# Edge tables built by node on ScalarE, and a group's product and sums moved within the step, in a graph attention and mixture-of-experts kernel

## The chip, the core and the metric

One Trainium2 chip, one of its cores. The metric is device time of the whole kernel in microseconds; smaller is better. Engines are named as in the profile: PE (TensorE matmul), PEld (its weight load), DVE (VectorE), ACT (ScalarE), POOL (GpSimd), SP (SyncE, which here issues most DMAs).

## What is computed

6250 nodes with 256 features, 100,000 edges sorted by target node `dst`, so that a target's edges lie together. First a graph attention layer with 8 heads, then a routed feed-forward net with 8 experts of which each node uses 2. Cut to what matters here:

```python
h = (layer_norm(x) @ W).reshape(N, 8, 32)
e = leaky_relu(a_src[src] + a_dst[dst], 0.2)        # per edge and head
ee = exp(e - emax[dst])
agg = segment_sum(h[src] * (ee / segment_sum(ee, dst)[dst])[:, :, None], dst)
out = layer_norm(agg + xn @ W_res + bias)
x = x + out + gelu_tanh(out @ ffn_w1 + b1) @ ffn_w2 + b2   # per node
x = x + sum over the node's 2 experts of weight * expert(layer_norm(x))
```

Targets are drawn so that few edges per node lie at high node numbers and many at low ones.

## The kernel before

**Preparation (to about 121 us).** Node features go through the first norm and the product with `W`; per tile of 128 nodes a row of 256 features and 16 source factors goes to the DRAM table `tab_s`, and 16 target factors to `tab_d`, of which `tab_q` is an overlapping copy in windows of 32 nodes. The edge lists are turned so that a column holds 128 edges.

**The edge loop.** Edges are worked in 196 steps of four tiles of 128 edges. A step's four tiles belong to four windows of 32 neighbouring target nodes. One to eight steps form a group, whose four windows are summed together: there are 110 groups, of one step each at high node numbers, where the loop begins, and of two, four and eight further on. By the rule that forms the groups, the first 68 steps are groups of one step. What one step needs is spread over seven turns of the loop, by the table `STAGES` (L910), which gives each function the number of turns it lags behind, in the order in which a turn writes them:

```python
STAGES = ((sum_up, 6), (weigh, 3), (add_tiles, 4), (place, 4), (turn_spread, 1), (give, 2),
          (spread, 0), (add_nodes, 5), (fetch, 0))
```

- `fetch` (L806): four indirect gathers on POOL bring the source rows of 512 edges into `gs` (four buffers).
- `spread` (L817): DVE compares each edge's place in its window with 0..31 and so makes a one-hot table `oh`, a row for each edge. In a group's first step it also makes `qd` (L828), the group's target factors `gd` laid out in four blocks by a multiplication with `quad`.
- `turn_spread` (L832): PE transposes `oh` into the PSUM tile `pt`, and ACT copies it to `oht` (L836): the same table with a row for each node. `pt` is one buffer, shared with the transposes of the tasks (`turn`, L963).
- `give` (L839): PE multiplies `oht` and `qd` and so gives each edge its target's factors, `pz`.
- `weigh` (L846): DVE multiplies source and target factors (`ww`) and then the source rows by them (`msg`, L854).
- `add_tiles` (L860): PE sums `msg` into the four windows, `pl`; behind a group's last step ACT copies it to `part` (L873).
- `place` (L884): behind a group DVE makes the one-hot table `oh2` (L887) that moves the group's 128 rows to their places in a tile of nodes. `add_nodes` (L891) multiplies by it on PE into `p2` (L894, one buffer), and `sum_up` (L898) adds `p2` into the sums of two tiles of nodes on DVE (L905).

`fetch_nodes` (L787) gathers the target factors of 32 groups at once, writes them to DRAM as `tab_g` and reads them back by SP as `gd`; four such loads serve the kernel.

**The tasks.** Between these stages a planner (`run_tasks`, L937) puts the rest of the net: products of the residual weights (L1147), the nodes' dense net (`net`, L996, with L981 and L991) as soon as all edges of two tiles are summed, the choice of experts, the scattering of nodes into expert lists `xs` (L1351, POOL), and then blocks of 256 nodes of one expert, whose weights of 1 MB each come by SP (L1396, L1397) ahead of use and whose result is added into the output by an indirect DMA (L1436, POOL). Every task has an engine, a cost in us and the tasks that it needs. In each turn of the loop the planner takes tasks in order while the engine has room; the room is `ROOM` less what `EDGES` and, behind a group's end, `BEHIND` say that the stages need. Within a turn the stages are written first and the tasks after them, and each engine executes in that written order. Expert blocks that found no room in the loop are done after its end, in a tail (53 blocks in all).

```python
ROOM = {"PE": 7.5, "DVE": 7.6, "ACT": 5.0, "POOL": 2.6, "SP": 1e9}
EDGES = {"PE": 1.3, "DVE": 2.0}
BEHIND = {"PE": 0.5, "DVE": 1.4}
```

Of the kernel before, what the change touches and what calls it, by code (L numbers as in the profile page):

```python
# [47 lines left out]
P = 128  # L51
# [6 lines left out]
G = 4  # L58
# [3 lines left out]


ROOM = {"PE": 7.5, "DVE": 7.6, "ACT": 5.0, "POOL": 2.6, "SP": 1e9}
EDGES = {"PE": 1.3, "DVE": 2.0}
BEHIND = {"PE": 0.5, "DVE": 1.4}
ROOM_AFTER = {"PE": 7.7, "DVE": 7.0, "ACT": 7.0, "POOL": 5.2, "SP": 1e9}

QUEUE = 40.0
# [149 lines left out]
def gnn_moe_kernel(  # L219
# [66 lines left out]
    NG = len(order)  # L286
    NCH = -(-EP // P)
    NCW = -(-NW // P)
    DUMMY = NP


# [25 lines left out]
    res_d = dp.tile([NP, D], F32, name="res_d")  # L317
    xp_d = dp.tile([NP, D], F32, name="xp_d")
    xt_d = dp.tile([NT, P, KD * P], F32, name="xt_d")
    xs = dp.tile([E * CAP + BT, DX], F32, name="xs")  # L320

    tab_a = dp.tile([NP + P, H], F32, name="tab_a")
# [9 lines left out]
    loct = gp.tile([P, EP], F32, name="loct")  # L332
    srce = gp.tile([P, EP], I32, name="srce")
    snloc = gp.tile([P, NQ], F32, name="snloc")
    here = gp.tile([P, 2, NQ], F32, name="here")
    kfi = gp.tile([P, NQ], I32, name="kfi")
    qrow = gp.tile([P, NCW], I32, name="qrow")
# [50 lines left out]
    nc.gpsimd.memset(blank.bitcast(I32)[:, :, D:D + 1], int(BIG))  # L388
    number = cp.tile([P, NT], I32, name="number")
    nc.gpsimd.iota(number, pattern=[[P, NT]], base=0, channel_multiplier=1)  # L390

    quad = cp.tile([P, G], F32, name="quad")
    nc.vector.memset(quad, 0.0)
    for j in range(G):
        nc.vector.memset(quad[j * W32:(j + 1) * W32, j:j + 1], 1.0)
    prm = cp.tile([P, NPR], F32, name="prm")
    pe = cp.tile([P, E, KF + 2 * KD], F32, name="pe")
    wr_sb = cp.tile([P, KD, E], F32, name="wr_sb")
# [49 lines left out]
    with ExitStack() as actx:  # L448
# [94 lines left out]
        tmp = ap_.tile([P, NCH, P], F32, name="tmp")  # L543
        nc.vector.tensor_copy(drf, drow)
        nc.vector.tensor_copy(srf, srow)
        ends = ap_.tile([P, 2, NCH], F32, name="ends")
        nc.vector.tensor_copy(ends[:, 0], drf[:, :, 0])
        nc.vector.tensor_copy(ends[:, 1], drf[:, :, P - 1])
# [67 lines left out]
        for j in range(G):  # L616
            q = slice(j * W32, (j + 1) * W32)
            nc.vector.tensor_scalar(sn[q], first[q, :, j], pcol[q], float(-j * W32), op0=ALU.add,
                                    op1=ALU.add)
        nc.vector.tensor_sub(sn, sn, kff)  # L620
        nc.vector.tensor_scalar(snloc, sn, float(P), float(-P), op0=ALU.is_ge, op1=ALU.mult)
        nc.vector.tensor_add(snloc, snloc, sn)
        nc.vector.tensor_sub(sn, first[:, :, 0], kff)
        nc.vector.tensor_scalar(here[:, 0], sn, pcol, None, op0=ALU.is_le)
        nc.vector.tensor_scalar(here[:, 1], sn, pcol, None, op0=ALU.is_gt)
# [41 lines left out]
        nc.vector.tensor_scalar(stmp, srct, float(DUMMY), good, op0=ALU.subtract, op1=ALU.mult)  # L667
        nc.vector.tensor_scalar(srce, stmp, float(DUMMY), None, op0=ALU.add)

        nc.vector.memset(acc_hi[:, NT - KHI, :], 0.0)  # L670
        nc.vector.memset(acc_hi[:, 0:2, :], 0.0)
        nc.sync.dma_start(tab_s[NP:, :], zeros[:, :DT])
# [95 lines left out]
    fb2_bc = bcast(ffn_b2[None, :], "fb2_bc", D, fp)  # L768


    GC = P // G
    cw = gnn.enter_context(tc.tile_pool(name="cw", bufs=2))
    cps = gnn.enter_context(tc.tile_pool(name="cps", bufs=1, space=PSUM))
    l2b_bc = cw.tile([P, 2, D], F32, name="o", bufs=1)
# [7 lines left out]


    live = {}
    gds = {}

    def fetch_nodes(c):  # L787

        gq = bw.tile([P, W32 * 2 * H], F32, name="gq", bufs=1)
        nc.gpsimd.indirect_dma_start(  # L790
            out=gq, out_offset=None, in_=tab_q,
            in_offset=bass.IndirectOffsetOnAxis(ap=qrow[:, c:c + 1], axis=0))
        nc.sync.dma_start(tab_g[c * P:(c + 1) * P, :], gq)
        n = min(GC, NQ - c * GC)
        gd = bw.tile([P, GC, 2 * H], F32, name="gd")
        nc.sync.dma_start(gd[:, :n], tab_g[c * P:c * P + n * G, :].rearrange(
            "(g j) (r c) -> (j r) g c", j=G, r=W32))
        gds[c] = gd

    def step_tiles(s, a):  # L800

# [14 lines left out]

    def spread(s):  # L817

        q, i = order[s]
        oh = bw.tile([P, G, W32], F32, name="oh", bufs=6)  # L820
        nc.vector.tensor_tensor(oh, jrow[:, None, :W32].to_broadcast([P, G, W32]),
                                step_tiles(s, loct)[:, :, None].to_broadcast([P, G, W32]),
                                op=ALU.is_equal)
        live[s, "oh"] = oh
        if i == 0:
            qd = bw.tile([P, G, 2 * H], F32, name="qd", bufs=3)
            gd = gds[q // GC][:, q % GC, :]
            nc.vector.tensor_tensor(qd, gd[:, None, :].to_broadcast([P, G, 2 * H]),  # L828
                                    quad[:, :, None].to_broadcast([P, G, 2 * H]), op=ALU.mult)
            live[q, "qd"] = qd  # L830

    def turn_spread(s):  # L832
        po = cps.tile([P, KD, 2 * P], F32, name="pt")
        nc.tensor.transpose(po[:, 0, :P], live[s, "oh"].rearrange("p j r -> p (j r)"), ident)  # L834
        oht = bw.tile([P, P], F32, name="oht")
        nc.scalar.activation(oht, po[:, 0, :P], AF.Copy)  # L836
        live[s, "oht"] = oht

    def give(s):  # L839

        pz = bps.tile([P, G * 2 * H], F32, name="pz", bufs=2)
        nc.tensor.matmul(pz, live.pop((s, "oht")), live[order[s][0], "qd"].rearrange(
            "p j c -> p (j c)"), start=True, stop=True)
        live[s, "pz"] = pz

    def weigh(s):  # L846
# [36 lines left out]
    @behind_group  # L883
    def place(q):  # L884

        oh2 = bw.tile([P, P], F32, name="oh2")
        nc.vector.tensor_scalar(oh2, jrow[:, :P], snloc[:, q:q + 1], None, op0=ALU.is_equal)  # L887
        live[q, "oh2"] = oh2

    @behind_group  # L890
# [7 lines left out]
    def sum_up(q):  # L898
# [4 lines left out]
        for b in range(2):  # L903
# [3 lines left out]

    STAGES = ((sum_up, 6), (weigh, 3), (add_tiles, 4), (place, 4), (turn_spread, 1), (give, 2),  # L910
              (spread, 0), (add_nodes, 5), (fetch, 0))
    LASTST = 6


# [560 lines left out]
    notes = []  # L1475
    blocks, stored, cleared, sure, chunked, moew, last_hi, ahead = [], [], [], [], [0], [], [], []
    EARLY = 10
    final_list, there = [], None
    s, u, since, was_nodes = 0, 0, [], False

    with tc.manual_schedule():
        nc.sync.dma_start(xs[E * CAP:, :].rearrange("(p r) d -> p r d", r=2), blank[:, :2])
        while s < NG + LASTST or pending or u < len(units) or len(blocks) < NS:
            for g in range(s, min(s + EARLY, NG)):
                if order[g][0] // GC not in gds:
                    fetch_nodes(order[g][0] // GC)
            for f, d in STAGES:
                if 0 <= s - d < NG:
                    f(s - d)
            if s == NG + LASTST:  # L1490
                edges.close()
            if len(firsts) < len(units) and len(firsts) <= s + 1:
                first_unit(len(firsts))
            if len(firsts) == len(units) and firsts[-1].step is not None and fp:
                first_.close()
                fp = None
            if last_hi and last_hi[0].step is not None and not moew and not fp:
                hi_pool.close()
                moew.append(ctx.enter_context(tc.tile_pool(name="moew", bufs=2, side="right")))
            nb = len(blocks) + len(ahead)  # L1500
            if moew and len(ahead) < 2 and nb < NS and any(n > nb for n, _ in sure):
                block_loads(nb)

            while sum(t.cost for t in pending if t.eng == "PE") < QUEUE:
                if (u < len(units) and units[u][2] <= s - LASTST
                        and not (ahead and was_nodes)):
                    was_nodes = True
                    node_unit(u)
                    since.append(u)
                    u += 1  # L1510
                    if u % 2 == 0 or u == len(units):
                        chunk_tasks(since, u == len(units), u == len(units) - 1)
                        since = []
                elif ahead:
                    was_nodes = False
                    block_unit(*ahead.pop(0))
                else:
                    break
            room = dict(ROOM if s < NG + LASTST else ROOM_AFTER)
            if s < NG + LASTST:  # L1520
                g = s - 5
                ends = 0 <= g < NG and order[g][1] == groups[order[g][0]][1] - 1
                for e in EDGES:
                    room[e] -= EDGES[e] + ends * BEHIND[e]
            run_tasks(s, room)
            s += 1
            if there is None and final_list and final_list[0].step is not None and len(blocks) > NS - 2:
                there = nc.values_load(total[0:1, 0:1], min_val=0, max_val=NB)
        if NS < NB:
            with tc.If(there > NS):  # L1530
                while pending or len(blocks) < NB:
                    nb = len(blocks) + len(ahead)
                    if len(ahead) < 2 and nb < NB:
                        block_loads(nb)
                    if ahead:
                        block_unit(*ahead.pop(0))
                    run_tasks(s, dict(ROOM_AFTER))
                    s += 1
# [31 lines left out]
```

## Time and profile before

| | |
|---|---|
| runs of the kernel | 2172.37, 2181.78, 2203.38 us, median 2181.78 us |
| the profiled execution | 1972.14 us, span of its instructions 1970.4 us |
| mean granted TensorE clock in it | 0.926 |
| preparation, edge loop, tail in it | 0 to 121 us, 121 to 1592 us, 1592 to 1970 us |
| PE busy | 1634.8 us (83%) |
| POOL busy | 1122.1 us (57%) |
| DVE busy | 1078.1 us (55%) |
| ACT busy | 707.7 us (36%) |

The profiled execution was about 10% shorter than the runs, so a number from the profile says how the time is made up, and not what a run takes. A line of the groups reads: source line, engine, operation, tile written and tiles read, shape and count, then busy time and mean length of one, then the idle time of the engine ahead of them and what ended it.

### The profile page before, as it was taken

What the parts mean: (1) busy time and instruction counts of PE and PEld (TensorE: products, weight loads), DVE (VectorE), ACT (ScalarE), POOL (GpSimd) and SP (SyncE); (2) the same over time, 40 slices, a digit from 0 to 9 for tenths busy, and PEclk for the clock granted to TensorE, in tenths of its full rate; (3) what the DMA queues carried; (4) which work ended last, traced back from release to release, by engine and by line L of the source; (5) the groups of instructions that cost most, each with busy time, mean ns of one, the idle gap of its engine ahead of it and who ended that gap; (6) DMA issues with size and microseconds to landing.
All of it is one profiled execution on the core that took longest, in us unless ns stands there. A gap on an engine that the chain in (4) does not pass through costs nothing. (4 is left out here: it accounts for less than half of the span.)

```text
span 1970.4 us, 28382 instructions
## 1 busy us (share of the span) xinstructions
PE 1634.8 (83%) x8533; PEld 1250.6 (63%) x8533; DVE 1078.1 (55%) x3964; ACT 707.7 (36%) x1590; POOL 1122.1 (57%) x1165
## 2 busy tenths in 40 slices
PE   4835797778787988999899997996998949999997
PEld 3523565555555766766677765775776737777775
DVE  8836878877878775565667655462453501200000
ACT  3821232322233343344434342433334314333332
POOL 2027765655655767577778777777777722112122
PEclk8968899887887999999999998998999979999999
DMA  4967664644535456566564776576776655565652
GB/s 129 290 210 225 187 202 130 184 134 146 158 112 194 152 152 170 149 199 168 179 200 136 210 206 200 155 220 201 201 232 169 205 184 131 179 186 171 196 161 57
DMA packets 245260, 348.24 MB, mean 177 GB/s; under 512 B 46465, under 2 KB 200353, under 8 KB 245100
## 3 DMA queue, kind: packets, MB, share of 16 engines
q1 hardware_dynamic: 182476, 203.56, 31.8%
q0 software_dynamic: 59312, 139.32, 27.1%
q10 hardware_dynamic: 3312, 3.48, 0.6%
q8 instruction: 70, 1.15, 0.2%
q14 instruction: 90, 0.74, 0.1%
HBM read 282.90 MB, written 67.66 MB: 178 GB/s over the span
## 5 line engine op out<-in xcount | busy, mean ns | idle before, releaser
L812 POOL DMA_INDIRECT gs<-tab_s,srce x784 | 809.9, 1033 | 363.9 <-issue 198.9
L981 PE MATMUL ph<-turned_in,w1b 128*128 128x256 f32 x1696 | 400.3, 390 | 51.2 <-ACT ht L984 38.2
L991 PE MATMUL py<-w2b,ht 128*128 128x256 f32 x1696 | 382.6, 384 | 11.7 <-DVE lg L1121 6.2
L981 PEld LDWEIGHTS ph<-turned_in,w1b 128*128 128x128 f32 x1696 | 305.2, 193 | 124.4 <-ACT ht L984 57.4
L991 PEld LDWEIGHTS py<-w2b,ht 128*128 128x128 f32 x1696 | 325.0, 193 | 58.4 <-DVE lg L1121 7.7
L1436 POOL DMA_INDIRECT out_dram<-yb,to x106 | 176.9, 1668 | 312.5 <-ACT yb L1432 124.5
L984 ACT ACTIVATE ht<-ph,pc 128x256 f32<-128x256 f32 x424 | 198.4, 473 | 206.1 <-PE ph L981 205.6
L854 DVE TENSOR_TENSOR msg<-gs,msg 128x1024 f32<-128x1024 f32 x196 | 240.5, 1227 | 6.7
L1426 DVE TENSOR_TENSOR yb<-py,b2b 128x512 f32<-128x512 f32 x53 | 36.6, 690 | 360.4 <-PE py L991 276.8
L991 PE MATMUL py<-w_sb,ht 128*128 128x256 f32 x784 | 190.5, 405 | 17.3 <-DVE lg L1121 15.0
L981 PE MATMUL ph<-turned_in,w_sb 128*128 128x256 f32 (+1 forms) x800 | 192.5, 394 | 14.2 <-ACT ht L984 14.2
L991 PEld LDWEIGHTS py<-w_sb,ht 128*128 128x128 f32 x784 | 158.7, 205 | 46.4 <-DVE lg L1121 19.6
L981 PEld LDWEIGHTS ph<-turned_in,w_sb 128*128 128x128 f32 x800 | 150.4, 200 | 44.6 <-ACT ht L984 20.3
L873 ACT ACTIVATE part<-pl 128x264 f32<-128x264 f32 x110 | 42.9, 390 | 322.3 <-PE pl L869 319.6
L836 ACT ACTIVATE oht<-pt 128x128 f32<-128x128 f32 x196 | 53.9, 275 | 271.5 <-PE pt L834 214.8
L869 PE MATMUL pl<-msg,oh 128*32 128x264 f32 x1568 | 130.9, 406 | 17.1 <-DVE msg L854 17.0
L1351 POOL DMA_INDIRECT xs<-xe,slot x98 | 103.4, 1055 | 54.3 <-DMA xs<-blank 22.1
L894 PE MATMUL p<-part,oh 128*128 128x264 f32 x220 | 84.3, 469 | 59.5 <-DVE acc_hi L905 38.8
L984 ACT ACTIVATE ht<-ph,prm 128x256 f32<-128x256 f32 (+1 forms) x200 | 92.2, 469 | 113.0 <-PE ph L981 112.6
L834 PEld LDWEIGHTS pt<-ident,oh 128*128 128x128 f32 x196 | 27.6, 141 | 138.3 <-issue 81.0
L834 PE MATMUL pt<-ident,oh 128*128 128x128 f32 x196 | 65.5, 334 | 49.6 <-ACT turned_in L973 23.1
L973 ACT ACTIVATE turned_in<-pt,pc 128x256 f32<-128x256 f32 x106 | 53.9, 559 | 134.4 <-PE pt L966 124.1
(325 smaller groups left out, 1900.8 us busy)
## 6 DMA issues: line engine op xcount, KB each, us to landing
w1b<-in_L_ffn_W_dram SPq DMA_DIRECT2D x53, 1024.0 KB
w2b<-in_L_ffn_W_dram SPq DMA_DIRECT2D x53, 1024.0 KB
xb<-xs SPq DMA_DIRECT2D x53, 260.0 KB
gs<-tab_s,srce POOLq DMA_INDIRECT x784, 3.3
b2b<-in_L_ffn_b_dram SPq DMA_DIRECT2D x53, 128.0 KB
tab_s<-hg SPq DMA_DIRECT2D x12, 544.0 KB
xg<-in_x_dram SPq DMA_DIRECT2D x12, 512.0 KB
xt_d<-xt SPq DMA_DIRECT2D x12, 512.0 KB
```

Of the source, the lines that this page charges most:

```text
L812: nc.gpsimd.indirect_dma_start(out=gs[:, j, :], out_offset=None, in_=tab_s, in_offset=bass.IndirectOffsetOnAxis(ap=srce[:, t:t + 1], axis=0))
L834: nc.tensor.transpose(po[:, 0, :P], live[s, "oh"].rearrange("p j r -> p (j r)"), ident)
L836: nc.scalar.activation(oht, po[:, 0, :P], AF.Copy)
L854: nc.vector.tensor_tensor(msg[:, :, :D].rearrange("p t (h d) -> p t h d", h=H), gs[:, :, :D].rearrange("p t (h d) -> p t h d", h=H), msg[: ...
L869: nc.tensor.matmul(pl[j * W32:(j + 1) * W32, :], oh[:, j, :], msg[:, j, :], start=i == 0, stop=last)
L894: nc.tensor.matmul(p2, oh2, part, start=True, stop=True)
L973: nc.scalar.activation(xt[:, k, :n * P], pt[:, k, :n * P], AF.Identity, bias=scale[:, KD + k:KD + k + 1], scale=scale[:, k:k + 1])
L981: nc.tensor.matmul(ph[:, :W], w1[:, k, c * P:(c + 1) * P], env["in"][:, k, :W], start=k == 0, stop=k == KD - 1)
L984: nc.scalar.activation(ht[:, :W], ph[:, :W], func, bias=b[:, c:c + 1], scale=1.0)
L991: nc.tensor.matmul(env["py"][:, j, :], env["ht", c][:, j * P:(j + 1) * P], w2[:, c, :], start=c == 0, stop=c == KF - 1)
L1351: st = nc.gpsimd.indirect_dma_start(out=xs, out_offset=bass.IndirectOffsetOnAxis(ap=slots[k][:n, t:t + 1], axis=0), in_=xes[u // 2][:n, pl ...
L1436: nc.gpsimd.indirect_dma_start(out=out, out_offset=bass.IndirectOffsetOnAxis(ap=env["to"][:, j:j + 1], axis=0), in_=env["yb"][:, j, :], in ...
```

## The change

It has four parts.

1. The table by node, `oht`, is no longer a transpose of `oh`. The target node of every edge is stored in DRAM in the preparation (`dst_d`). Each step, SP loads the four rows of 128 node numbers, each row into 32 partitions (`load_dst`, one turn ahead of `spread` and two ahead of the table), and ACT makes the table as relu(1 - |dst - node|) with two activations (`is_node`). `turn_spread` is gone, and `spread` comes one turn later.
2. `oh2` is made in the same way by ACT in place of DVE.
3. `qd` is no longer made by DVE. Three buffers of four groups' factors each are cleared once; SP loads the factors straight into the four blocks, four DMAs for four groups (`fetch_factors`). `fetch_nodes` is called at the same distance as before.
4. `sum_up` comes after `weigh`, `add_tiles`, `place`, `give` and `spread` in the turn, and `add_nodes` after the turn's tasks. `EDGES` and `BEHIND` get smaller values, so that the planner has more room for tasks.

```diff
-EDGES = {"PE": 1.3, "DVE": 2.0}
-BEHIND = {"PE": 0.5, "DVE": 1.4}
+EDGES = {"PE": 0.95, "DVE": 2.0}
+BEHIND = {"PE": 0.5, "DVE": 1.0}
...
+    node = gp.tile([P, NQ], F32, name="node")
+    qds = [gp.tile([P, GC, G, 2 * H], F32, name=f"qd{i}") for i in range(QB)]
...
+        nc.sync.dma_start(dst_d.rearrange("(c t) e -> t c e", t=P), drf)
...
+    def fetch_factors(c):
+        n = min(GC, NQ - c * GC)
+        for j in range(G):
+            nc.sync.dma_start(
+                qds[c % QB][j * W32:(j + 1) * W32, :n, j, :], bass.AP(
+                    tensor=tab_g.tensor,
+                    offset=tab_g.offset + (c * GC * G + j) * W32 * 2 * H,
+                    ap=[[2 * H, W32], [G * W32 * 2 * H, n], [1, 2 * H]]))
...
-        if i == 0:
-            qd = bw.tile([P, G, 2 * H], F32, name="qd", bufs=3)
-            gd = gds[q // GC][:, q % GC, :]
-            nc.vector.tensor_tensor(qd, gd[:, None, :].to_broadcast([P, G, 2 * H]),
-                                    quad[:, :, None].to_broadcast([P, G, 2 * H]), op=ALU.mult)
-    def turn_spread(s):
-        po = cps.tile([P, KD, 2 * P], F32, name="pt")
-        nc.tensor.transpose(po[:, 0, :P], live[s, "oh"].rearrange("p j r -> p (j r)"), ident)
+    def load_dst(s):
+        q, i = order[s]
+        t0, m = groups[q]
+        rows_ = bg.tile([P, P], F32, name="rows_")
+        nc.sync.dma_start(rows_, bass.AP(tensor=dst_d.tensor, offset=dst_d.offset + (t0 + i) * P,
+                                         ap=[[m * P, G], [0, W32], [1, P]]))
+    def is_node(out, rows_, less):
+        nc.scalar.activation(out, rows_, AF.Abs, bias=less)
+        nc.scalar.activation(out, out, AF.Relu, bias=1.0, scale=-1.0)
+    def spread_by_node(s):
+        q, i = order[s]
         oht = bw.tile([P, P], F32, name="oht")
-        nc.scalar.activation(oht, po[:, 0, :P], AF.Copy)
+        is_node(oht, live.pop((s, "rows")), node[:, q:q + 1])
...
-        nc.vector.tensor_scalar(oh2, jrow[:, :P], snloc[:, q:q + 1], None, op0=ALU.is_equal)
+        is_node(oh2, jrow, snloc[:, q:q + 1])
...
-    STAGES = ((sum_up, 6), (weigh, 3), (add_tiles, 4), (place, 4), (turn_spread, 1), (give, 2),
-              (spread, 0), (add_nodes, 5), (fetch, 0))
+    STAGES = ((weigh, 3), (add_tiles, 4), (spread_by_node, 1), (place, 4), (give, 2), (spread, 1),
+              (sum_up, 6), (load_dst, -1), (fetch, 0))
...
             run_tasks(s, room)
+            if 0 <= s - 5 < NG:
+                add_nodes(s - 5)
```

The pool `bg` of `rows_` has four buffers. In the written order of the changed kernel, 46 of the products of the expert blocks (L981, L991, of 1696 in all) and 8 of their transposes stand in the loop that stood in the tail before.

## The prediction

> **What bounds the kernel now.** I first read the span by stages, with the busy time of PE, PEld, DVE, ACT and POOL in each, since the share over the whole span mixes preparation, edge loop and tail.
>
> ```profile
> 0.00:121.00 121.00, 76.44 (x329) 53.95 (x329) 97.65 (x516) 74.10 (x206) 15.65 (x73) 0.93 0.66 206
> 121.00:200.00 79.00, 31.68 (x170) 20.20 (x170) 39.29 (x108) 7.01 (x23) 53.70 (x51) 0.72 0.78 225
> 200.00:650.00 450.00, 354.92 (x1813) 258.30 (x1811) 364.43 (x1297) 133.69 (x305) 279.15 (x302) 0.86 0.54 160
> 650.00:1200.00 550.00, 502.42 (x2776) 387.09 (x2777) 351.04 (x1267) 222.44 (x473) 401.05 (x407) 0.98 0.60 174
> 1200.00:1592.00 392.00, 347.24 (x1961) 265.24 (x1959) 181.09 (x579) 142.20 (x312) 289.41 (x271) 0.96 0.67 199
> 1592.00:1971.00 379.00, 322.05 (x1488) 265.86 (x1488) 44.62 (x199) 128.22 (x272) 83.15 (x64) 0.94 0.54 158
> ```
>
> Call the four stages of the loop A, B, C, D, and the tail E. In B, PE (79%) and DVE (81%) are equally loaded and neither is full: they wait for each other. In C and D, PE is 91% and 89% busy. POOL is fuller there than it looks: each gather is followed by some 0.3 us in which POOL waits for nothing that the profile shows.
>
> ```profile
> POOL gs L812 <- issue: 57.4, 190, 0.3
> ```
>
> That is stage D; with 8.3 us of the same kind before its other indirect DMAs, POOL is taken for 289 + 66 = 355 of 392 us. In C it is 401 + 88 = 489 of 550. A is bound by the first gathers, E by PE.
>
> Next I read the groups of instructions (page, part 5) for what the change touches, and those of the loop on DVE.
>
> ```profile
> L836 ACT ACTIVATE oht<-pt 128x128 f32<-128x128 f32 x196 | 53.9, 275 | 271.5 <-PE pt L834 214.8
> L894 PE MATMUL p<-part,oh 128*128 128x264 f32 x220 | 84.3, 469 | 59.5 <-DVE acc_hi L905 38.8
> L834 PE MATMUL pt<-ident,oh 128*128 128x128 f32 x196 | 65.5, 334 | 49.6 <-ACT turned_in L973 23.1
> ```
>
> ```profile
> L887 DVE TENSOR_SCALAR oh<-jrow,snloc 128x128 f32<-128x128 f32 x110 | 31.2, 283 | 0.0
> L828 DVE TENSOR_TENSOR qd<-gd,quad 128x64 f32<-128x64 f32 x110 | 23.9, 218 | 19.5 <-DMA gd<-tab_g 19.5
> ```
>
> PE spends 65.5 us on the transposes and stands 49.6 us before them; it stands 59.5 us before the group's product, because `p2` is one buffer and `sum_up` of the same turn has to empty it. The waits of PE in B show how much of this lies there:
>
> ```profile
> PE p L894 <- DVE acc_hi L905: 38.5, 15, 5.3
> PE p L894 <- DVE acc_lo L905: 16.4, 5, 7.1
> ```
>
> So 54.9 of B's 95.1 idle PE us are this wait. Last I read SP's own waits, because the change puts a load into its queue in every step:
>
> ```profile
> SPq L1397 <- PE py L991: 241.9, 34, 17.1
> SPq L1404 <- DMA xs<-xe,slot: 236.5, 15, 34.1
> SPq L1094 <- DVE xin L1071: 209.3, 15, 39.9
> ```
>
> SP often stands for long at the head of its queue, and what is written behind it waits too.
>
> **What the Trainium skill says.** "ScalarE: Activation LUTs", section "What ACT_TABLE_LOAD costs", prices an activation with immediate scale and bias at 186 ns + 0.833 ns for each element of the row, 93 ns more for a bias by partition, and has back-to-back ones overlap by 93 ns. For 128 elements that is 293 ns for a plain one; the copy at L836 took 275, so the trace agrees. The same page, "Table sets: the hidden batching unit", says that relu and abs are in every set: the new activations switch no table, and the written order agrees (55 table loads against 57); no trace of before shows these two functions. "DMA: Bandwidth & Descriptors", section "Queues, rings and completion order", says that SP has one row of rings and that each DMA engine takes a ring's descriptors in order. A small load behind expert weights then waits for them. The trace of before fits: after a pair of weight loads is issued (2.1 MB) SP's queue moves packets for about 10 us.
>
> **The change, part by part**, against the profiled execution of 1972 us.
>
> *Table by node.* Taken from PE: 196 transposes, 65.5 us busy (4.3, 19.3, 24.0, 17.9 in A to D), and the waits around the shared PSUM tile: 23.1 us before L834, and by the same list of waits some 8 us in C before the tasks' transposes. On ACT the copy of 0.275 us becomes two activations: abs with a bias by partition, estimate 0.39 us, and relu, 0.29 to 0.39, less 0.09 of overlap: 0.59 to 0.69, I take 0.65. So 196 x 0.38 = 74 us more on ACT, if the second adds no wait for the first (the upper bound, 0.1 us each, adds 20).
>
> *Table of the group.* 110 x 0.283 = 31 us leave DVE, and 110 x 0.65 = 72 us come to ACT. ACT's load in B goes from 134 to 134 + 57 x 0.38 + 57 x 0.65 = 193 of 450 us, in C from 222 to 273 of 550, in D from 142 to 169 of 392. It stays half idle, and the work lies after `part`, which waits for PE in any case. I price it at nothing; the cover gone (ACT late with `ht`, two buffers of `ph`), its 146 us would show in part.
>
> *Factors.* 23.9 us leave DVE. SP issues 112 DMAs instead of 4. At the start 12 of them stand ahead of the first row loads: 12 issues of about 0.5 us (L796's took 0.37, with 0.2 between issues) and one landing more. Before, the first `pz` came 5.8 us after `gd` was issued; I charge 4 us in A. Later ones come some turns early and cost nothing.
>
> *Row loads.* 196 loads of 64 KB (12.8 MB beside 348) with two turns from issue to use. Bounded above from the trace: I took the last SP issue ahead of the place where each load will stand and compared it with the moment two turns later at which ACT made that table. The median distance is 26 us, the least 3.3, and 4 of 194 are under 9 us. Four buffers hold the load back until ACT has used the one four steps before. If each load also had to wait until SP's queue next ran empty, plus 2.5 us, 18 would be late, in 11 places, 96 us of ACT's time at most, nearly all in C and D where `xb` and the weights stand ahead. Below it is nothing. I take 14 us: queues seldom have to run empty, and PE has two buffers of `ph` before it feels ACT.
>
> *Order in the turn.* `add_nodes` now stands behind the tasks, so `sum_up` has most of a turn in hand and the 58 us of waits at L894 go. In exchange `sum_up` can start only when PE has finished the turn before, and DVE's tasks stand behind it. DVE's `weigh` stands ahead of it, and PE needs only that for its next turn. So a step's DVE work has about two turns, and I charge nothing; some of the 58 us will come back as other waits between these two.
>
> *Room.* The written order moves 46 products (400.3 + 382.6 us for 1696, 0.46 each) and 8 transposes (0.27) from E into the loop: 23 us.
>
> **The sum by stages.**
> - A: 4 us longer.
> - B: PE 355 - 19 = 336, DVE 364 - 57 x 0.50 = 336. With all 61 us of removed waits gone, 336 + 95 - 61 = 370; with all of them back, 431. I take 408, since DVE is as loaded as PE: 42 us shorter.
> - C: PE 502 - 24 + 12 moved in = 490, and 28 of its 48 idle us stay: 518. POOL needs 489, so both are over 93% full; I add 6: 524, 26 shorter.
> - D: PE 347 - 18 + 11 = 340, idle 45 less 12: 373; POOL needs 355; I take 376, 16 shorter.
> - E: 23 shorter. Late rows: 14 longer.
>
> 42 + 26 + 16 + 23 - 4 - 14 = 89, so 1972 becomes 1883, a ratio of 0.955. The runs' median was 2181.78, 10.6% over the profiled execution, and no view tells why. I apply the ratio: 2083 us (taking off 89 us would give 2093).
>
> **The rivals.**
> - *Rows late.* ACT stands at its abs behind a row load that lies behind `xb` or 2.1 MB of weights, with every `ht` behind it. For: SP's waits of up to 34 us, and 32 blocks' weights loaded within the loop. Against: the median of 26 us. It cancels the other 103 us when the 32 loads cost PE over 3.2 us each; at 6 us each the profile is 1972 - 103 + 192 = 2061, the runs 2280: slower.
> - *POOL or ACT is the bound in C and D.* POOL's work is the same, so C and D give 5 us each, and B half of mine: 21 + 10 + 23 - 4 - 14 = 36, runs 2142: within 2%. For: POOL at 89 and 91% there. Against: the gathers run up to three turns ahead.
> - *The waits simply go.* B 370, C 505, D 360, no row late: 80 + 45 + 32 + 23 - 4 = 176, runs 1987. For: PE's granted clock of 0.86 in B against 0.98 in C; "TensorE: Matmul & The Clock Gate", section "Part 1: The HAM clock gate", has the clock fall after idle stretches, so fewer gaps would pay twice. Against: DVE, at 81% there, has waits of its own.
> - *The change doesn't do what it says*: the waits at L894 stay because DVE lags by more than a turn. Then only the removed work counts, about 50 us, runs 2126.
>
> **How the numbers follow.** Forecast 0.53 (2040 to 2130), waits go 0.12, POOL or ACT bound 0.20, rows late 0.11, waits stay 0.04. A difference of 2% is about what a measurement of this kernel can tell. Faster: 0.53 + 0.12 + 0.03 + a quarter of the POOL case = 0.73. Slower: 0.10. Within 2%: 0.17. The range leaves out half of the fast case and most of the slow one: 2025 to 2185.
>
> **What would show it.** Right: no wait for `sum_up` before the group's product on PE; DVE down by about 55 us; ACT up by about 146; B near 408 us and the tail near 356; no table loads around abs. Wrong: long waits of ACT for the row loads (`rows_`), PE standing before L981 for more than the 65 us (51.2 + 14.2) of the page before, or POOL without free time in C and D. A loop that takes as long as before would refute the sum.

## The result, and the profile after

The changed kernel takes 2245.65 us (median of 4 runs, 2235.97 to 2250.04), the kernel before beside it 2185.1 us (2172.37 to 2203.38): ratio 1.0267, 95% interval [1.0219, 1.0315]. It is slower; 2083 us were forecast.

Its profiled execution is one of these runs (2235.97 us, span 2234.2 us), while that of before took 1972 us. So the two profiles must not be subtracted from each other. On some chips the kernel before takes 1975 to 1977 us, on others 2155 to 2194; the runs of the result are of the second kind. I call the second kind *late chips*, for a reason shown below. Two chips of each kind were met in the experiments; only one of them was met twice, half an hour apart, and was of the first kind both times, so whether it is the chip or something of the hour is not shown. Beside e17 and e18 the kernel before spread from 2124 to 2161 us, and their ratios count its faster runs alone; by the medians of all runs they would be 1.011 and 1.002. The profile to set beside the one shown ahead is that of the changed kernel run once more on a chip of the first kind (experiment e5, 1975.19 us, span 1973.4 us). Its busy times in the windows used before, with the columns PE, PEld, DVE, ACT, POOL, then the TensorE clock:

```profile
0.00:121.00 121.00, 75.25 (x329) 53.54 (x329) 98.96 (x512) 73.13 (x204) 16.18 (x73) 0.93 0.66 203
121.00:200.00 79.00, 28.12 (x141) 17.98 (x142) 30.49 (x69) 15.06 (x48) 46.46 (x47) 0.68 0.77 219
200.00:650.00 450.00, 344.15 (x1713) 251.79 (x1711) 337.42 (x1139) 180.51 (x458) 268.79 (x291) 0.85 0.58 167
650.00:1200.00 550.00, 496.55 (x2680) 379.76 (x2681) 341.78 (x1234) 274.08 (x625) 398.31 (x412) 0.97 0.64 184
1200.00:1592.00 392.00, 349.51 (x1922) 267.32 (x1921) 183.61 (x584) 170.96 (x396) 303.02 (x279) 0.95 0.75 212
1592.00:1971.00 379.00, 333.83 (x1557) 273.56 (x1555) 51.06 (x211) 130.00 (x277) 82.24 (x66) 0.96 0.55 159
```

The same windows of the profiled run of the result, where the loop ends near 1880 us:

```profile
200.00:650.00 450.00, 321.60 (x1536) 231.55 (x1537) 298.33 (x972) 161.31 (x416) 233.97 (x251) 0.84 0.50 146
650.00:1200.00 550.00, 425.95 (x2124) 318.63 (x2122) 299.66 (x1087) 221.12 (x505) 318.44 (x337) 0.88 0.54 154
1200.00:1592.00 392.00, 311.79 (x1553) 232.40 (x1554) 175.92 (x600) 143.67 (x336) 232.54 (x239) 0.88 0.55 158
```

In e5 PE is busy for 344 us of B, where it was 355; 19 us of transposes had been charged there. In C and D it is busy for 497 and 350 us, where it was 502 and 347. So hardly any of PE's time was freed. In the run of the result, where every window holds less of the work, PE is busy for 322, 426 and 312 us: there the engines wait longer for each other.

**What became of the waits.** The waits of PE before the group's product in B, of e5:

```profile
PE p L915 <- DVE acc_hi L926: 11.2, 3, 7.2
PE p L915 <- DVE acc_lo L926: 9.4, 2, 6.3
```

They fell from 54.9 (49.5 in e1, the kernel before once more) to 20.6 us, as forecast. But now VectorE stands before its sums. The same window, VectorE, e5, and below it e1:

```profile
DVE acc_hi L926 <- PE p L915: 73.1, 22, 7.0
DVE acc_lo L926 <- PE p L915: 11.2, 2, 5.8
```

```profile
DVE xin L1071 <- PE py L991: 21.3, 6, 5.0
DVE acc_hi L905 <- PE p L894: 13.6, 4, 4.6
DVE acc_hi L905 <- issue: 12.8, 20, 1.0
DVE acc_lo L905 <- issue: 3.8, 6, 0.7
```

84.3 us against 13.6 that are put down to the product, or 35.5 with all waits before the sums. And behind these sums on VectorE stand the tasks whose results PE needs; of e5's PE in B:

```profile
PE py L1169 <- issue: 36.6, 9, 5.7
PE py L1013 <- DVE lg L1143: 18.7, 9, 6.6
...
PE py L1135 <- DVE lg L1143: 6.5, 1, 6.5
PE py L1135 <- DVE pos L1306: 4.3, 3, 2.8
```

The first line names no releaser, but the trace shows one: each of the nine waits ends 0.10 us after VectorE's L1175 (eight times) or L1093 (once) has read the PSUM tile `py`, which is one buffer, and straight ahead of that instruction VectorE did the two sums of the group. All waits of PE before a product into `py` come to 77.1 us in B, where e1 had 32.0. The gathers wait for VectorE as before (`gs` behind `oh`, 106.3 us in B, where it was `msg` with 98.9).

**The lines of the moved tables**, e5:

```profile
L849 ACT ACTIVATE oht<-oht 128x128 f32<-128x128 f32 x196 | 60.7, 310 | 6.2
...
L848 ACT ACTIVATE oh<-jrow,snloc 128x128 f32<-128x128 f32 x110 | 42.4, 386 | 0.0
...
L849 ACT ACTIVATE oh<-oh 128x128 f32<-128x128 f32 x110 | 34.0, 310 | 3.5
```

0.39 + 0.31 = 0.70 us a table, where I took 0.65: the 0.09 us of overlap that the estimate took off is not there. The relu reads what the abs wrote, and in e5 it starts 0.03 us after the abs has ended (median of 306 pairs), whereas other neighbours on ACT do overlap, by 0.09 us in the median. ACT is busy 843.7 us instead of 707.6 (136 more; 146 forecast). SP's longest wait is new, and it made no row load late after the start:

```profile
SPq L842 <- ACT oht L849: 211.3, 49, 10.3
```

SP stands at a row load until ACT has freed a row buffer. ACT itself waits for rows only at the start (29.4 and 6.2 us for the first ones) and under 1 us in all afterwards.

**Why these chips are called late.** The trace of the run of the result holds the moments at which PE's count of finished work rose, for 1328 of its 1515 counted instructions. 165 of them lie over 0.5 us after the end of the latest recorded product; merged, these are 71 stretches of 209 us together, the longest 13.8. (Measured from the end of the latest product that itself raises the count they are 124 stretches of 303 us, the longest 16; the 117 and 297 in the expectation of e14 are of this looser kind.) In e5, with 1514 moments, there is one, after the last product. Both traces hold the same 8337 matmul instructions, so no lost records of products explain the stretches. VectorE's and ACT's counts show hardly any (6.3 and 1.0 us in all), though part of their moments is missing too (2414 of 3310 and 1386 of 1820 are there). Mean lengths agree (`msg` takes 1228 ns in both). The Trainium skill, "Perfetto Trace Analysis", section "Tensor Engine Instruction (MATMUL, LD_WEIGHTS)", says that the end of a matmul in a profile is estimated from its size and is no measurement; this agrees. A place in the run of the result, 1080 to 1110 us, by the list of waits:

```profile
ACT part L894 <- remote: 17.1, 1, 17.1
...
PE py L1013 <- issue: 12.1, 1, 12.1
DVE acc_lo L926 <- remote: 11.9, 1, 11.9
```

By the records PE ended its last product at 1092.7 us; its count rose at 1102.3, and until then PE, ACT and VectorE all stood. In such gaps the granted clock halves (here from 1094.6 us on, for 13.7 us): 531 us at half clock against 316 in e5, of which 240 against 75 between 650 and 1600 us. The time behind the last `weigh` is no longer than on the other chips (363 us against 372 in e5), so it is the loop that suffers. What holds PE there no view tells.

### The profile page after: what moved, and what is told of

It is laid out like the page before. It is cut to its first block, busy times and chain, and to the rows that moved or that the text cites. A ratio compares the mean times of both kernels' runs of the same rounds, so it can differ in the third digit from the quotient of the medians.

```text
span 2234.2 us, 28501 instructions
## 1 busy us (share of the span) xinstructions
PE 1716.8 (77%) x8337; PEld 1291.9 (58%) x8337; DVE 1044.6 (47%) x3744; ACT 842.9 (38%) x2004; POOL 1099.7 (49%) x1165
## 3 DMA queue, kind: packets, MB, share of 16 engines
q1 hardware_dynamic: 210988, 216.87, 30.6%
## 5 line engine op out<-in xcount | busy, mean ns | idle before, releaser
L824 POOL DMA_INDIRECT gs<-tab_s,srce x784 | 788.2, 1005 | 627.2 <-DVE oh L832 396.8
L1003 PE MATMUL ph<-turned_in,w1b 128*128 128x256 f32 x1696 | 443.4, 417 | 119.0 <-ACT ht L1006 69.5
L1003 PEld LDWEIGHTS ph<-turned_in,w1b 128*128 128x128 f32 x1696 | 327.7, 207 | 213.3 <-ACT ht L1006 94.5
L1013 PE MATMUL py<-w2b,ht 128*128 128x256 f32 x1696 | 395.5, 393 | 43.8 <-DVE top L1146 15.5
L1003 PE MATMUL ph<-turned_in,w_sb 128*128 128x256 f32 (+1 forms) x800 | 217.9, 426 | 70.9 <-ACT ht L1006 42.7
L875 DVE TENSOR_TENSOR msg<-gs,msg 128x1024 f32<-128x1024 f32 x196 | 240.7, 1228 | 7.2 <-DVE msg L874 0.5
L1003 PEld LDWEIGHTS ph<-turned_in,w_sb 128*128 128x128 f32 x800 | 162.8, 216 | 112.2 <-ACT ht L1006 52.6
L894 ACT ACTIVATE part<-pl 128x264 f32<-128x264 f32 x110 | 42.9, 390 | 388.7 <-PE pl L890 143.2
L871 DVE TENSOR_TENSOR ww<-gs,pz 128x64 f32<-128x64 f32 x196 | 43.0, 219 | 251.2 <-PE pz L863 103.7
L926 DVE SCALAR_TENSOR_TENSOR acc_lo<-p,here,acc_lo 128x264 f32 x112 | 55.1, 492 | 207.3 <-PE p L915 113.4
L863 PEld LDWEIGHTS pz<-qd,oht 128*128 128x128 f32 x392 | 63.5, 203 | 127.7 <-issue 117.2
L863 PE MATMUL pz<-qd,oht 128*128 128x64 f32 x392 | 91.3, 316 | 35.7 <-DMA rows__1862<-dst_d 32.9
```

The lines of the kernel that those rows point to most:

```text
L824: nc.gpsimd.indirect_dma_start(out=gs[:, j, :], out_offset=None, in_=tab_s, in_offset=bass.IndirectOffsetOnAxis(ap=srce[:, t:t + 1], axis=0))
L863: nc.tensor.matmul(pz, live.pop((s, "oht")), qd.rearrange("p j c -> p (j c)"), start=True, stop=True)
L871: nc.vector.tensor_tensor(ww, gs[:, :, D:], live.pop((s, "pz")).rearrange("p (j c) -> p j c", j=G), op=ALU.mult)
L875: nc.vector.tensor_tensor(msg[:, :, :D].rearrange("p t (h d) -> p t h d", h=H), gs[:, :, :D].rearrange("p t (h d) -> p t h d", h=H), msg[: ...
L926: nc.vector.scalar_tensor_tensor(to, p2, here[:, b, q:q + 1], to, op0=ALU.mult, op1=ALU.add)
L1003: nc.tensor.matmul(ph[:, :W], w1[:, k, c * P:(c + 1) * P], env["in"][:, k, :W], start=k == 0, stop=k == KD - 1)
```

## The experiments

Ratios are to the kernel before on the same chip, with 95% intervals; they are formed from the single runs and can differ by some 0.3 points from the ratio of the medians given. e1 to e8 and e13 to e16 ran where it takes 1975 to 1977 us, e9 to e12 (2193.65) and e17, e18 (2155.33) on late chips.

**e1 and e5: both kernels as they are.**

> The kernel before, unchanged, for a second profile. The profiled execution of before took 1972 us where its runs took 2172 to 2203. If that execution was an odd one (TensorE unhindered in it), the profile here has a span near 2180 us with longer waits for PE. If profiling itself shortens it, the span is again near 1970 us. The ratio to the kernel before is 1.00 in both cases.

> The changed kernel, unchanged. The kernel before took 2185 us beside it and 1977 us in the runs of the other experiments, with the same instructions: something outside the program slowed it by 10%. If the loss of 2.7% is the program's own (the order, which cost 1.6% when made alone in the kernel before, less the 1.1% that the rest gained), the ratio here is 1.00 to 1.02 where before takes about 1977 us. If it comes only with what slowed those runs, the ratio is 0.97 to 0.995 here.

e1: 1977.8 us, 1.0009 [0.9996, 1.0022]. e5: 1976.68 us, 0.9998 [0.9979, 1.0016]. Off the late chips the whole change is worth nothing, neither way. And the kernel before takes some 1977 us there in all its runs (1966 to 1984 in those of e1), so it is not the profiling that made the execution shown ahead short.

**e2: the changed kernel with the order of before.**

```diff
-    STAGES = ((weigh, 3), (add_tiles, 4), (spread_by_node, 1), (place, 4), (give, 2), (spread, 1),
-              (sum_up, 6), (load_dst, -1), (fetch, 0))
+    STAGES = ((sum_up, 6), (weigh, 3), (add_tiles, 4), (spread_by_node, 1), (place, 4), (give, 2),
+              (spread, 1), (add_nodes, 5), (load_dst, -1), (fetch, 0))
...
-            if 0 <= s - 5 < NG:
-                add_nodes(s - 5)
```

> The changed kernel with the order of before: sum_up first in the turn, add_nodes among the stages. If the new order is the cause of the loss (DVE waits for the group's product behind all tasks of PE's turn, and POOL's gathers wait for DVE), this is at 0.97 to 0.99 of before. If the row loads and what they do to SP's queue are the cause, it stays at 1.02 to 1.04.

1957.39 us, 0.989 [0.9869, 0.991]. The tables, factors, loads and room gain 1.1%, and the order takes that away.

**e3: the kernel before with the order of the change alone** (`STAGES` and the place of `add_nodes` as in the change, everything else as before).

> The kernel before with nothing but the new order of sum_up and add_nodes. If the order is the cause: 1.03 to 1.06 of before. If it is not: 0.98 to 1.00, since the wait of PE for sum_up goes.

2012.07 us, 1.0159 [1.0137, 1.018]. The order alone loses, by about half of the least that I expected. VectorE's wait shows at the instruction that now needs the end of PE's turn first: `place`, here still VectorE's, whose table's buffer the product frees (200 to 650 us):

```profile
DVE oh L887 <- PE p L894: 81.1, 23, 7.2
```

**e6 and e7: one of the two moves each.** e6 keeps the product ahead of the tasks and the sums behind `weigh`; e7 keeps the sums first and the product behind the tasks.

```diff
 e6
-              (sum_up, 6), (load_dst, -1), (fetch, 0))
+              (sum_up, 6), (add_nodes, 5), (load_dst, -1), (fetch, 0))
...
-            if 0 <= s - 5 < NG:
-                add_nodes(s - 5)
 e7
-    STAGES = ((weigh, 3), (add_tiles, 4), (spread_by_node, 1), (place, 4), (give, 2), (spread, 1),
-              (sum_up, 6), (load_dst, -1), (fetch, 0))
+    STAGES = ((sum_up, 6), (weigh, 3), (add_tiles, 4), (spread_by_node, 1), (place, 4), (give, 2),
+              (spread, 1), (load_dst, -1), (fetch, 0))
```

> The changed kernel with add_nodes ahead of the tasks again, as the last stage, and sum_up left behind weigh. If the product behind the tasks is what costs (its result comes at the end of PE's turn and DVE stands for it): within 1% of e2, so 0.98 to 1.00 of before. If sum_up behind weigh costs (PE stands for it): 1.00 to 1.02.

> The changed kernel with sum_up first in the turn again, and add_nodes left behind the tasks. DVE then stands at the head of its turn until PE has ended the turn before. If that wait is what costs, this is the worst of all: 1.03 to 1.08. If it is hidden, it is at 0.98 to 1.00.

e6: 1938.33 us, 0.981 [0.9759, 0.986]; e7: 2079.56 us, 1.0515 [1.0464, 1.0566]. With e2 and e5 this is a square. The sums behind `weigh` gain in either place of the product (0.989 to 0.981, or 0.9856 to 0.9826 in the repeats e16 and e15, and 1.0515 to 0.9998); the product behind the tasks loses in either place of the sums (0.981 to 0.9998, 0.989 to 1.0515). In e7 VectorE, 200 to 650 us:

```profile
DVE acc_hi L926 <- PE p L915: 124.3, 28, 9.1
```

There `weigh` itself stands behind that wait, and all of PE's edge work behind `weigh`. In e6 VectorE has no wait for `p` at all, PE's wait is back and longer than before, and the time is shorter all the same:

```profile
PE p L915 <- DVE acc_hi L926: 45.7, 15, 6.4
PE p L915 <- DVE lg L1143: 15.9, 5, 6.1
PE p L915 <- DVE acc_lo L926: 9.1, 3, 6.6
PE p L915 <- DVE tot L1303: 7.3, 2, 4.6
```

All waits of over 0.15 us in B, in us, added up from the traces:

| wait in B | e1 | e2 | e5 | e6 | e7 |
|---|---|---|---|---|---|
| PE before the group's product (`p`) | 49.5 | 58.1 | 20.7 | 80.7 | 5.8 |
| PE before products of tasks into `py` | 32.0 | 28.4 | 77.1 | 0.9 | 112.3 |
| VectorE before its sums | 35.5 | 36.0 | 84.3 | 0.3 | 134.3 |

PE's two waits together come to 81.5 us in e1 and to no clearly less in any order (81.6 in e6, 79.4 in its repeat e15): the change moved them from the group's product to the tasks. e6 gains on e2 in PE's busy time, not in its idle time: in the first 57 steps PE is idle for 84.3 against 86.1 us and busy for 308.9 against 322.0, with nearly as many products (1595 and 1602), at a mean granted clock of 0.877 against 0.847; in the repeats 85.0 against 87.6, 310.0 against 320.6, and 0.866 against 0.860. Why is not shown.

**e4 and e8: two other parts undone.** e4 makes `oht` by PE's transposes again, without row loads, with `EDGES` 1.3 for PE; e8 has `EDGES` and `BEHIND` of before.

```diff
 e4
+        nc.tensor.transpose(po[:, 0, :P], live[s, "oh"].rearrange("p j r -> p (j r)"), ident)
+        nc.scalar.activation(oht, po[:, 0, :P], AF.Copy)
-        is_node(oht, live.pop((s, "rows")), node[:, q:q + 1])
 e8
-EDGES = {"PE": 0.95, "DVE": 2.0}
-BEHIND = {"PE": 0.5, "DVE": 1.0}
+EDGES = {"PE": 1.3, "DVE": 2.0}
+BEHIND = {"PE": 0.5, "DVE": 1.4}
```

> The changed kernel with the table by node made by transposes on TensorE as before, so without row loads (and with PE's EDGES of 1.3). If the row loads are the cause: 0.96 to 0.99 of before. If the order is: 1.03 to 1.06, as the 65 us of transposes come back to PE.

> The changed kernel with EDGES and BEHIND of before, so fewer tasks in a turn. If the fuller turns are what costs: 0.98 to 1.00 of before. If they gain a little as forecast: up to 1% slower than the changed kernel.

e4: 1991.89 us, 1.0061 [1.0039, 1.0082], between its two ranges; e8: 1991.87 us, 1.0083 [1.0058, 1.0109]. Against e5 the room is worth 0.8% (from their runs 1.0082, [1.0066, 1.0099]), and table by node and room together 0.6%: without the room that comes with it, no gain of the table from row loads is seen in this order. The comparison is not quite clean, since e4 keeps the changed `BEHIND`, and as before `spread` one turn earlier and six buffers of `oh`. PE is busy for 1626.4 us in e8 and 1644.7 in e4, 18 us for the 196 transposes; in e8 it is idle for 16 us more.

**e9 to e11: more work for PE** (on a late chip), **e13 and e14: the same** (off it). Does the order cost more when PE's turn is longer? Two products of the first layer are issued once more in six of eight chunks, and overwritten:

```diff
+        for k in range(2 if c % 4 != 3 else 0):
+            nc.tensor.matmul(ph[:, :W], w1[:, k, c * P:(c + 1) * P], env["in"][:, k, :W],
+                             start=True, stop=True)
```

> The kernel before with 936 products more on TensorE (in six of eight chunks of each FFN's first layer the first two products are issued once more and overwritten), 0.22 us each by the page, 205 us: as much as the runs of the result lie above the profiled executions. The tasks' declared costs are as before. If TensorE carries the time, 1977 + 150 to 205, ratio 1.08 to 1.10. This is the base for the next two.

> The changed kernel with the same 936 products more. Theory (in the changed order VectorE's sums wait for the end of TensorE's turn, so a TensorE that needs longer for a turn costs the changed kernel more): 1.5 to 3.5% above the kernel before with the same products, as in the scored runs, ratio to the plain kernel before 1.10 to 1.13. Rival (the order's loss does not grow with TensorE's time; the scored runs differ by something else): within 0.7% of the kernel before with the same products.

> The changed kernel with the group's product ahead of the tasks and the sums behind weigh, and with the same 936 products more. Theory: without the sums' wait for the end of the turn it keeps its gain, 1.5 to 3% below the kernel before with the same products. Rival (any gain in waits is lost when TensorE needs longer, since TensorE is then full): within 0.7% of it.

> As e9: the kernel before with 936 products more. Beside a kernel before of about 1975 us it should take 150 to 205 us more, ratio 1.08 to 1.10. Beside one of about 2185 us 1.1077 again.

> As e10: the changed kernel with the same products. Beside a kernel before of about 1975 us: 1.5 to 3% above e13 if a TensorE that is longer busy in each turn is by itself what makes the changed order dearer; within 0.7% of e13 if it is ends of TensorE that come late without its being busy, as in the trace of the scored run (117 stretches, 297 us). Beside one of about 2185 us: 2.2% above e13 again.

e9 2428.85 us, 1.1077 [1.1036, 1.1117]; e10 2483.51 us, 1.1349 [1.129, 1.1409]; e11 2442.17 us, 1.1142 [1.1085, 1.12]; e13 2240.36 us, 1.1327 [1.1297, 1.1357]; e14 2270.1 us, 1.1488 [1.1457, 1.152]. The products took more than expected (off the late chip 264 us, 1976 to 2240): each is two instructions in the trace (PE has 1872 more), and the 0.22 us of the expectation are for one of them. PE's busy time rose by 367 us (1638.9 in e1 to 2006.3 in e13); 264 of them show in the time, the rest went into idle time. What counts is after against before with the same products (from the four runs of each): e14 to e13 1.0134 [1.0110, 1.0159], e10 to e9 1.0246 [1.0172, 1.0320]. So a longer turn of PE turns 1.000 into 1.013, somewhat under the 1.5% expected. VectorE's waits before its sums between 200 and 650 us grow with it, to 116.2 us in e14, where e5 had 84.3 (e13: 53.1, where e1 had 35.5):

```profile
DVE acc_hi L926 <- PE p L915: 109.6, 27, 8.7
DVE acc_lo L926 <- PE p L915: 6.6, 1, 6.6
```

e11 to e9 is 1.0059 [0.9988, 1.0131]: on the late chip the better order gains nothing on the kernel before. But e11 to e10 is 0.9818 [0.9736, 0.9899]: between the two orders of the changed kernel it gains as much as off late chips (1.9%, below). The trace of e9 shows late ends too, 42 stretches of 122 us, against 58 of 165 in e10 and 60 of 163 in e11, one run each (by the looser count 225, 236 and 247 us). So the kernel before is not free of them; whether the change brings more is not settled.

**e12: the group's table back on VectorE** (late chip), one comparison instead of two activations.

```diff
-        is_node(oh2, jrow, snloc[:, q:q + 1])
+        nc.vector.tensor_scalar(oh2, jrow[:, :P], snloc[:, q:q + 1], 0.0, op0=ALU.add,
+                                op1=ALU.is_equal)
```

> The changed kernel with the group's table again one comparison on VectorE (0.28 us, 31 us in all come back to it, 77 us leave ACT). Theory (VectorE's time is slack in the changed order, since it waits for TensorE's turn anyway): 0.998 to 1.004. The prediction's reading (half of what leaves VectorE in the first half pays): 0.5 to 1% slower than the changed kernel, 1.005 to 1.010. If ACT's longer table was itself late: 0.990 to 0.997.

2236.54 us, 1.0223 [1.0159, 1.0286], where the changed kernel had 1.0267 [1.0219, 1.0315] in the runs of the result. Giving VectorE its 31 us back costs nothing that shows; a loss of over half a per cent is unlikely, a small gain is not excluded. The expectation was written for chips of the other kind.

**e15 and e17, e16 and e18: e6 and e2 again**, to see them on a late chip; only the second pair met one.

> As e6: the changed kernel with the group's product ahead of the tasks and the sums behind weigh. Beside a kernel before of about 2185 us: theory (the product behind the tasks is the whole loss) 0.98 to 1.00; rival (the sums behind weigh cost there too, since VectorE stands at them while TensorE's end is late) 1.01 to 1.02. Beside one of about 1975 us 0.981 again.

> As e2: the changed kernel with the order of before. Beside a kernel before of about 2185 us: theory (the order is the loss, the other parts gain everywhere) 0.985 to 0.995; rival (the tables, the row loads and the room lose there) 1.01 to 1.03. Beside one of about 1975 us 0.989 again.

> The changed kernel with the group's product ahead of the tasks and the sums behind weigh. Beside a kernel before of about 2185 us: theory (the product behind the tasks is most of the loss) 0.99 to 1.01; rival (the sums behind weigh cost there) 1.015 to 1.03. Beside one of about 1975 us 0.982 again.

> The changed kernel with the order of before. Beside a kernel before of about 2185 us: theory (the order is the loss, the other parts gain everywhere) 0.985 to 0.998; rival (the tables, the row loads and the room lose there) 1.01 to 1.03. Beside one of about 1975 us 0.986 to 0.989 again.

e15: 1944.09 us, 0.9826 [0.9799, 0.9853]; e16: 1950.53 us, 0.9856 [0.9827, 0.9885]: e6 and e2 hold. On the late chip e17: 2178.13 us, 1.0204 [1.0071, 1.0338]; e18: 2159.53 us, 1.0137 [0.9976, 1.0298]. My theory, that the product behind the tasks is the whole difference between the chips, falls with e17: with the product ahead of the tasks the kernel still loses there. That the sums behind `weigh` cost there is not excluded: e17 to e18 is 1.0073 [0.9976, 1.0170]. e18 leaves both of its ranges open. In all three orders the changed kernel stands 2.7 to 3.8 points worse on late chips than off them (0.9998 to 1.0267, 0.9826 to 1.0204, 0.9856 to 1.0137, the last with an interval that leaves 1.2 to 4.4). So at least part of what is dearer there lies in what the three share.

## Why the prediction was wrong, step by step

The stretches between the starts of VectorE's `weigh`, in us, read from the traces of e1 (before), e5 (the change), e2 and e6:

| stretch | e1 | e5 | e2 | e6 |
|---|---|---|---|---|
| start to first `weigh` | 144.7 | 152.5 | 155.5 | 155.7 |
| steps 0 to 56 | 414.5 | 424.6 | 408.1 | 393.2 |
| steps 56 to 126 | 543.4 | 550.1 | 545.7 | 541.5 |
| steps 126 to 195 | 473.9 | 474.1 | 471.5 | 473.7 |
| last `weigh` to the end | 396.9 | 372.1 | 375.6 | 371.3 |

The forecast had the loop (A to D and late rows) 66 us shorter and the tail 23. In e5 the loop up to the last `weigh` became 25 us longer and the rest 25 shorter. Of the 89 us that are missing, two steps of the prediction explain most: the order in the turn, 38 us (e5 to e6), and the transposes, 53 us of PE's time that was never there. That the two come to about 89 is no proof, since busy time saved need not be time saved.

- *Order in the turn: this step failed.* The prediction said "a step's DVE work has about two turns, and I charge nothing". Both halves of its ground were true: `sum_up` can start only when PE has ended its turn, and DVE's tasks stand behind it. What was overlooked is that PE's tasks of the same turn need these tasks' results, or the PSUM buffer that they empty. So the two engines alternate: PE's tasks, the product, the sums, VectorE's tasks, PE's tasks again. "PE needs only that for its next turn", said of `weigh`, was the false sentence: PE's waits before tasks' products into `py` went from 32.0 to 77.1 us in B, and to 0.9 in e6. Price off the late chips: 1.1% against the order of before (e5 to e2), 1.9% against the best (e5 to e6, from their runs 1.0188, [1.0160, 1.0217]).
- *Table by node, "65.5 us busy" taken from PE: this term was mis-sized.* PE's busy time fell from 1638.9 (e1) to 1627.4 us in e5 and 1626.4 in e8, 12 us, and by 18 from e4 to e8. The busy times of groups of instructions overlap: those of PE sum to 1763 us in e1, where PE is busy for 1639. Without the transpose its neighbour shows more: the product `pz`, written next behind it, has 88.6 us of busy time in e5 where it had 66.6. So the 336, 490 and 340 us of PE's work in the sum were too low, and the gains of C and D went with them.
- *B, 42 us shorter.* Measured in the first 57 steps (from about 145 to 560 us): 10 longer; with the order of before 6 shorter; in e6 21 shorter. The waits at L894 did go (54.9 to 20.6 us), and more than that came back on VectorE (35.5 to 84.3).
- *C and D, 26 and 16 shorter.* No order gave more than 2.4 us in the two later stretches. PE's busy time in them hardly fell: 478.5 and 421.6 us in e1, 480.1 and 425.1 in e5 with the tasks moved in, 467.4 and 421.5 in e8 without them. The rival "POOL or ACT is the bound in C and D", with half of my gain in B, gives 1936 us against the profiled execution, and e6 and e15 took 1938 and 1944; but its sign, POOL without free time, is missing: in e6 POOL still waits 32.4 us for `oh` from 650 to 1200 us, while PE is busy for 501 of 550. I take the match for luck.
- *Tail and room, 23 us: right for the tail* (24.8). With the old room (e8) the tail is 29 us longer than in e5 and the loop 12 shorter; the room is worth 15 us, 0.8%.
- *Start, 4 us:* 7.8 to 11, since the first row load is waited for (29.4 us of ACT's time); in e4, without row loads, 4.0.
- *Tables on ACT at nothing: right off the late chips.* PE stands 61.4 us before L1003 in e5, 47.6 of them for `ht`, where the page before had 65.4 and 52.4. In C the wait for `ht` doubled (14.1 to 30.6 us), but with the same tables and the old room (e8) it is 18.1: most of that belongs to the fuller turns.
- *Late rows, 14 us, and the rival of that name: did not occur.* ACT's waits for rows after the start sum to under 1 us.
- *VectorE 55 us less:* the lengths of its instructions sum to 52 us less (1209.9 to 1158.1), but busy time fell by 33 (1076.3 to 1043.3), because neighbours overlap. In e12 the relief did not show in the time.
- *The ratio.* 0.955 was carried over from the profiled execution to runs that took 10.6% longer, for which "no view tells why". That was one more failed step: the change is worth 0.9998 on one kind of chip and 1.0267 on the other. The order does get dearer when PE's turn grows (e14), but on a late chip it costs about what it costs off it (1.8% from e11 to e10 on one chip, against 1.9%; 1.3 points from e18's 1.0137, on another, to 1.0267, against 1.1), so as far as these runs tell it does not explain the difference. Whether it is the tables, loads or room that lose there, and why, stays open. Not tried on such a chip: each part alone but the group's table, and a profile of the kernel before with nothing added. A conjecture that fits but was not tested is that ACT's tables, which stand behind `part` and so behind PE's late end, are late with it.

Off the late chips e6 beats both kernels by 1.7 to 1.9% (with e15); on them no variant was faster than the kernel before.

## What to carry to other kernels

When two stages are moved apart to remove a wait, follow both queues once round: what stands behind the moved consumer, who needs that, and whether it leads back to the moved producer; a consumer at the front of one engine's tasks, fed by a producer at the back of the other's, makes them alternate. Undo the two halves of such a move separately, since here one gained and the other lost. The busy time of a group of instructions overlaps with its neighbours', so what taking the group away frees is read from the engine's busy time with and without it (here 12 to 18 us for 65). And where a profile and the runs it stands for differ by 10%, the forecast is for the profile only; a ratio need not carry over.

## What the runs showed of the hardware

- The same kernel takes 1975 to 1977 us on some chips and 2155 to 2194 us on others. On the latter PE's count of finished work rises up to 13.8 us after the recorded end of its last product, 209 us in 71 stretches of the run of the result, while VectorE's and ACT's counts show 6.3 and 1.0 us; half-clock time is 531 us, where e5 has 316. The loop is slowed, the stretch after it is not (363 against 372 us).
- Abs with a bias by partition took 386 to 393 ns and relu with immediate scale and bias 310 ns for 128x128, and neither added table loads (55 in all against 57). A relu that reads the abs ahead of it starts 0.03 us after its end; other neighbours on ACT overlap by 0.09 us.
- 936 products of 128x256 more (1872 instructions) made PE busy for 367 us more and the kernel 264 us longer (e13).
